# A hybrid attention and spectral kernel: the last stage placed inside the spectral stage, the rest loaded at once, columns loaded by GpSimd's queue, first matrices ahead of the token points

## The chip, the cores and the metric

The kernel runs on one core of one Trainium2 chip. The metric is the device time of one launch in microseconds (us). Each time is from one run; the median of three is compared. A profile is one execution recorded by the hardware profiler. Engines are named as the profile names them: PE is TensorE (PEld its weight loads), DVE is VectorE, ACT is ScalarE, POOL is GpSimd, SP is SyncE, which here only issues DMAs. ACT and POOL can issue DMAs as well.

## The reference

An image of 4 x 56 x 56 tokens with 128 channels passes a neighbourhood attention layer (group norm, 7 x 7 windows), a linear attention layer, and then a spectral layer, where the change lies. Cut to the spectral layer:

```python
t = t + attention(layer_norm(t))            # t: 4 x 3136 x 128
u = layer_norm(t)
for i, frac in enumerate((1, 2, 4, 8)):      # one of the four is selected by the weights
    ui = u[:, :T // frac]
    U_plus  = causal_fft_conv(phi, ui)       # 16 filters
    U_minus = sign * causal_fft_conv(phi, ui * sign)
    s_i = einsum('btkd,k,kde->bte', U_plus, sigma**0.25, M_phi_plus[i])
    s_i += einsum('btkd,k,kde->bte', U_minus, sigma**0.25, M_phi_minus[i])
    s_i += sum_j einsum('btd,de->bte', shift(ui, j), M_u[i, j])   # j = 0, 1, 2
out = t + sum_i weights[i] * pad(s_i)
```

All is float32.

## The kernel before

The program has three stages, one after the other: `layers` (both attention layers, the short shifts with M_u, and all preparation for the spectral layer), `spectral_layer`, and `onto_the_rest`. A second copy of all three stands in a branch that these inputs don't take.

`layers` leaves in HBM: `td`, the tokens with everything added but the spectral part (this is "the rest"); `xd`, the normalized tokens transformed along the image rows into 42 frequencies m1 (real and imaginary parts, and two shifts s); `vd`, the transformed filters; `wd`, the selected filter matrices (32 x 128 x 128). Its order is planned in Python by estimated costs and is then fixed on every engine.

`spectral_layer` goes over the 42 row frequencies, singly at both ends and in pairs between (`UNITS`). Four pieces of work make one frequency:

- Token points (L1490): `xm`, four loads from `xd` (L1478), is multiplied by the table `tok`. DVE, ACT and POOL copy the result into `us`, twelve planes (L1499 to L1503). Three `us` buffers are used in turn.
- Matrices (L1521): the 2 MB of `mats`, loaded once from `wd` by four DMAs on SP (L1433), times the filter points `v`, eight blocks t to a frequency. DVE and ACT copy them into `gt` (L1531).
- Products (L1541): `gt` times `us`, copied by ACT into `ys` (L1633). `ys` goes to `yd` in HBM and comes back regrouped as `yg` (L1554, L1560).
- Columns (L1569): `yg` times the table `back`, copied by ACT and DVE into `zs` (L182, L184), stored to `zd` in HBM by four DMAs on SP (L1584).

The function `step` writes the order on PE by hand: the matrices of the next unit are made between the products of the present one. For the very first unit there are no products: it makes the token points, and then all eight blocks of matrices. The results of the last frequency come after the last product.

The tables `v`, `tok` and `back` come in chunks of six frequencies on SP (L1463). SP works its list in order. A load into a buffer waits until the old content is used, and the DMAs of SP and ACT take eight semaphores in turn, so each also waits until the DMA that last had its semaphore has landed.

`onto_the_rest` transforms back along the rows. It opens its buffers when `spectral_layer` has closed its own. It clears `onto` and eight `z` buffers (four deep, two image halves q; L1687, L1697, DVE and POOL share the clearing), as the 84 rows that are loaded (partitions 0 to 83) are multiplied as 128. Then eleven steps of 1, 1, 2, 4, 4, 4, 4, 4, 2, 1, 1 image columns follow. In each, and for both halves:

- `tl`, the rest for these columns, is loaded from `td` by ACT (L1709), four buffers deep;
- `z` is loaded from `zd` by SP (L1711), 4 KB for each row and column;
- PE multiplies (L1719), four matmuls a column, each recorded twice;
- DVE masks and adds the result into `tl` (L1728), and ACT stores `tl` to the output (L1733).

In all, `z` is 19.3 MB, the rest 6.4 MB and the output 6.4 MB.

Of the kernel before, what the change touches and what calls it, by code (L numbers as in the profile page):

```python
# [57 lines left out]
NS, BR = 2, H // 2  # L58
N1, N2, NM = 42, W, W // 2
# [74 lines left out]
def hybrid_kernel(  # L134
# [39 lines left out]
    hmask = keep.tile([P, 1], F32, name="hmask")  # L174
# [1244 lines left out]
    def spectral_layer():  # L1419


        with ExitStack() as ph:
            tabs = ph.enter_context(tc.tile_pool(name="tabs", bufs=2))
            sp = ph.enter_context(tc.tile_pool(name="sp", bufs=2))
            sp1 = ph.enter_context(tc.tile_pool(name="sp1", bufs=1))
            ps_g = ph.enter_context(tc.tile_pool(name="ps_g", bufs=1, space=bass.MemoryType.PSUM))


# [1 line left out]
            mats = sp1.tile([P, NQE, GE // NQE, C], F32, name="mats")  # L1430
            by_group = wd.rearrange("k (t g i) d -> g k t (i d)", t=NQE, g=NG)
            for g in range(NG):
                nc.sync.dma_start(  # L1433
                    mats[32 * g : 32 * (g + 1)].rearrange("k t i d -> k t (i d)"), by_group[g]
                )

# [151 lines left out]
            def bank():  # L1588
                turn[0] = (turn[0] + 1) % 8
                return ps_g.tile([P, 512], F32, tag=f"g{turn[0]}", name="pg")  # L1590
# [19 lines left out]
            def step(s):  # L1610


                one = UNITS[s - 1] if s else []
                two = UNITS[s] if s < len(UNITS) else []
                turns = NM // 4
                free = MQ * len(one)

                order = list(range(free, NQE)) + list(range(free)) if two else []
                need = lambda t: -(-NMQ * (t + 1) // 4) if t < free else 0
                done = 0  # L1620

                def make():
                    if order and need(order[0]) <= done:
                        t = order.pop(0)
                        for n in range(len(two)):
                            matrices(s, t, n)

                def use(q, ns):

                    py = bank().rearrange("p (n c) -> p n c", c=C)  # L1630
                    for i, n in enumerate(ns):
                        product(py[:, i], s - 1, us_of(one[q]), q, n)
                    nc.scalar.copy(ys[:, ns[0] : ns[-1] + 1], py[:, : len(ns)])  # L1633

                if not one:
                    load_to(1)
                    points(0)
                    while order:
                        make()
                elif len(one) == 1 and two:  # L1640
                    ys = sp.tile([P, turns, C], F32, name="ys")
                    for n in range(turns):
                        make()
                        use(0, [n])
                        done += 1
                        if n == 3:
                            points(two[0])
                    ygs[one[0]] = regroup(one[0], ys)
                    make()
                    points(two[1])  # L1650
                else:
                    waiting = list(ygs)
                    for q in range(len(one)):
                        ys = sp.tile([P, turns, C], F32, name="ys")
                        for n in range(0, turns, 2):
                            last = n + 1 == turns
                            if last and q == 0 and two:
# [12 lines left out]
                assert not order  # L1670

            with tc.manual_schedule(engines={mybir.EngineType.PE}):
                for s in range(len(UNITS) + 1):
                    if s + 1 < len(UNITS):
                        tables_of(UNITS[s + 1][0])
                    step(s)
                for m1 in list(ygs):
                    results(m1)

    def onto_the_rest():  # L1680

        with ExitStack() as ph:
            fin = ph.enter_context(tc.tile_pool(name="fin", bufs=4, reuse_waits="tile"))
            ps_o = ph.enter_context(tc.tile_pool(name="ps_o", bufs=4, space=bass.MemoryType.PSUM))

            onto = fin.tile([P, NS, 64], F32, name="onto", bufs=1)
            nc.vector.memset(onto, 0.0)  # L1687
            nc.scalar.dma_start(
                onto[: 2 * N1, :, :H], table["onto"].rearrange("p (s h) -> p s h", s=NS)
            )  # L1690
            zs = [
                [fin.tile([P, 4, NS, B * C], F32, name=f"z{q}{i}", bufs=1) for q in range(2)]
                for i in range(4)
            ]
            for i in range(4):
                for q, e in enumerate((nc.vector, nc.gpsimd)):
                    e.memset(zs[i][q][64:], 0.0)  # L1697
            rows_in = td.rearrange("b (h w) c -> h b w c", w=W)
            rows_out = ot.rearrange("b (h w) c -> h b w c", w=W)

            steps = (1, 1, 2, 4, 4, 4, 4, 4, 2, 1, 1)
            assert sum(steps) == W // 2
            for n, wc in enumerate(steps):
                w0 = sum(steps[:n])
                tl = fin.tile([P, B, max(steps), C], F32, name="tl")
                zin = []
                for q in range(2):
                    ws = slice(q * BR + w0, q * BR + w0 + wc)
                    nc.scalar.dma_start(tl[64 * q : 64 * q + H, :, :wc], rows_in[:, :, ws])  # L1709
                    z = zs[n % 4][q]  # L1710
                    nc.sync.dma_start(  # L1711
                        z[: 2 * N1, :wc], zd[ws].rearrange("w p s b e -> p w s (b e)")
                    )
                    zin.append(z)
                for i in range(wc):
                    po = ps_o.tile([P, B, C], F32, name="po2")
                    for s in range(NS):
                        for q in range(2):
                            nc.tensor.matmul(  # L1719
                                po[64 * q : 64 * (q + 1)].rearrange("p b c -> p (b c)"),  # L1720
                                onto[:, s],
                                zin[q][:, i, s],
                                start=(s == 0),
                                stop=(s == NS - 1),
                            )
                    for q in range(2):
                        at = slice(64 * q, 64 * q + H)
                        nc.vector.scalar_tensor_tensor(  # L1728
                            tl[at, :, i], po[at], hmask[at], tl[at, :, i], ALU.mult, ALU.add
                        )  # L1730
                for q in range(2):
                    ws = slice(q * BR + w0, q * BR + w0 + wc)
                    nc.scalar.dma_start(rows_out[:, :, ws], tl[64 * q : 64 * q + H, :, :wc])  # L1733

    unfit = keep.tile([1, 1], mybir.dt.int32, name="unfit")
    layers(False, unfit)
    bad = nc.values_load(unfit)
    spectral_layer()
    onto_the_rest()
    with tc.If(bad > 0):  # L1740
        layers(True, None)
        spectral_layer()
        onto_the_rest()


# [52 lines left out]
```

## Time and profile before

| | us |
|---|---|
| median of 3 runs | 1634.19 (1628.76 to 1636.43) |
| the profiled execution | 1643.69 |
| its span, first to last instruction | 1641.8 |
| PE busy / DVE / ACT / POOL in it | 1436.1 / 1015.0 / 757.9 / 411.8 |
| spectral stage: first token load issued, last product starts | 757.53, 1486.23 |
| last columns (L1569) start | 1497.54 |
| first onto matmul (L1719), last one | 1518.25, 1635 |

The mean clock granted to PE is 0.939. Durations below are of the profiled execution, whose own time lies 9.5 us above the median of the runs. A line of a timeline has start, duration, engine, line, operation, and in brackets the idle time before it with what ended it. A line of the chain of waits has start, duration, and the instruction or wait that the chain passes through; "issue" is time for which the profile shows no cause. In the busy times by stage each engine has busy us and, in brackets, its number of instructions. "DMA share" is the mean busy share of 16 DMA engines; where packets overlap it can pass 1.

### The profile page before, as it was taken

What the parts mean: (1) busy time and instruction counts of PE and PEld (TensorE: products, weight loads), DVE (VectorE), ACT (ScalarE), POOL (GpSimd) and SP (SyncE); (2) the same over time, 40 slices, a digit from 0 to 9 for tenths busy, and PEclk for the clock granted to TensorE, in tenths of its full rate; (3) what the DMA queues carried; (4) which work ended last, traced back from release to release, by engine and by line L of the source; (5) the groups of instructions that cost most, each with busy time, mean ns of one, the idle gap of its engine ahead of it and who ended that gap; (6) DMA issues with size and microseconds to landing.
All of it is one profiled execution on the core that took longest, in us unless ns stands there. A gap on an engine that the chain in (4) does not pass through costs nothing.

```text
span 1641.8 us, 60848 instructions
## 1 busy us (share of the span) xinstructions
PE 1436.1 (87%) x26361; PEld 1115.2 (68%) x26361; DVE 1015.0 (62%) x2069; ACT 757.9 (46%) x1610; POOL 411.8 (25%) x813
## 2 busy tenths in 40 slices
PE   4887879889999999883999999999999999992566
PEld 3665658756876776562888888888888888880212
DVE  3775668777876777541766666666666666643324
ACT  2333445346635534342666655666566556640000
POOL 5135327433754464240010011001010101003000
PEclk9698999999999999996999999999999999995788
DMA  6455455744434244257144444444444454435997
GB/s 174 106 109 105 89 86 109 162 122 118 117 111 125 66 121 124 74 157 202 48 113 119 106 123 126 127 108 125 122 126 108 121 132 115 107 93 139 225 252 238
DMA packets 274388, 207.22 MB, mean 126 GB/s; under 512 B 104704, under 2 KB 241056, under 8 KB 274112
## 3 DMA queue, kind: packets, MB, share of 16 engines
q1 hardware_dynamic: 261154, 189.63, 45.1%
q10 hardware_dynamic: 12958, 13.61, 3.1%
q8 instruction: 209, 3.42, 0.9%
q14 instruction: 67, 0.55, 0.1%
HBM read 115.52 MB, written 87.64 MB: 124 GB/s over the span
## 4 chain that ended last, share of the span: by engine, by line
PE 66%; DMA 14%; POOL 7%; DVE 6%; SPq 4%; issue 2%; ACT 1%; POOLq 0%; DVEq 0%; ACTq 0%
PE pg L1521 18%; PE pg L1541 17%; PE pg L1490 5%; PE results L1185 4%; PE scores L1155 3%; PE pg L1569 3%; PE bk L828 3%; SPq L230 2%; DMA z<-zd 2%; DMA tl<-td 2%; DMA out_dram<-tl 2%; PE bk L887 2%; PE bk L733 2%; PE bk L703 2%; PE bk L501 2%
## 5 line engine op out<-in xcount | busy, mean ns | idle before, releaser
L1531 DVE COPY gt<-pg 128x448 f32<-128x448 f32 x672 | 372.9, 617 | 225.6 <-PE pg L1521 225.5
L1531 ACT COPY gt<-pg 128x448 f32<-128x448 f32 x672 | 313.6, 555 | 101.3 <-PE pg L1521 101.1
L1521 PE MATMUL pg<-v,mats 32*128 32x224 f32 (+1 forms) x5632 | 308.9, 356 | 0.0
L1541 PE MATMUL pg<-gt,us 128*32 128x128 f32 x9408 | 297.7, 277 | 1.3 <-DVE gt L1531 1.3
L1541 PEld LDWEIGHTS pg<-gt,us 128*32 128x32 f32 x9408 | 256.5, 138 | 51.8 <-DVE gt L1531 45.4
L1521 PEld LDWEIGHTS pg<-v,mats 32*128 32x128 f32 x5632 | 250.5, 187 | 30.0 <-issue 28.5
L1502 POOL COPY us<-us 128x448 f32<-128x448 f32 x42 | 23.5, 560 | 667.0 <-DVE us L1499 611.9
L1171 ACT ACTIVATE e<-scores 126x768 f32<-126x768 f32 (+1 forms) x140 | 107.6, 769 | 116.8 <-PE scores L1155 93.3
L1175 DVE TENSOR_TENSOR e<-e,relb 126x768 f32<-126x768 f32 (+1 forms) x140 | 138.1, 987 | 23.7 <-ACT e L1171 23.0
L1199 DVE RECIPROCAL recs<-results 128x96 f32<-128x96 f32 (+1 forms) x140 | 99.4, 710 | 55.1 <-PE results L1185 53.9
L1719 PE MATMUL po<-z,onto 128*64 128x512 f32 x224 | 76.6, 723 | 58.5 <-DMA z<-zd 57.4
L1155 PEld LDWEIGHTS scores<-qT,kp 32*126 32x126 f32 (+1 forms) x2240 | 75.3, 187 | 50.0 <-ACT e L1171 25.2
L1155 PE MATMUL scores<-qT,kp 32*126 32x96 f32 (+1 forms) x2240 | 98.2, 291 | 11.8 <-ACT e L1171 11.6
L1490 PE MATMUL pg<-tok,xm 56*128 56x56 f32 x1344 | 87.2, 278 | 24.3 <-DMA xm<-xd 24.3
L1633 ACT COPY ys<-pg 128x256 f32<-128x256 f32 (+1 forms) x171 | 58.6, 343 | 106.2 <-PE pg L1541 102.3
L1490 PEld LDWEIGHTS pg<-tok,xm 56*128 56x128 f32 x1344 | 81.5, 191 | 36.8 <-issue 25.4
L1719 PEld LDWEIGHTS po<-z,onto 128*64 128x64 f32 x224 | 25.3, 163 | 110.5 <-issue 75.9
L1499 DVE COPY us<-pg 128x448 f32<-128x448 f32 x84 | 48.5, 620 | 67.2 <-PE pg L1490 67.2
L1728 DVE SCALAR_TENSOR_TENSOR tl<-po,hmask,tl 56x512 f32<-56x512 f32 x56 | 42.0, 750 | 74.0 <-PE po L1719 73.3
L828 PE MATMUL bk<-mu,ut 128*112 128x128 f32 x672 | 82.3, 281 | 2.2 <-POOL ut L812 1.6
L1185 PE MATMUL results<-e,v_sb 126*32 126x96 f32 (+1 forms) x2240 | 76.1, 255 | 9.3 <-DVE aT L1200 9.3
L1214 POOL TENSOR_TENSOR total<-total,recs 128x448 f32<-128x448 f32 x28 | 31.7, 1134 | 206.4 <-DVE recs L1199 206.4
(176 smaller groups left out, 1969.1 us busy)
## 6 DMA issues: line engine op xcount, KB each, us to landing
xd<-xs SPq DMA_DIRECT2D x56, 336.0 KB
xm<-xd SPq DMA_DIRECT2D x168, 112.0 KB
yd<-ys SPq DMA_DIRECT2D x168, 112.0 KB
yg<-yd SPq DMA_DIRECT2D x168, 112.0 KB
zd<-zs SPq DMA_DIRECT2D x168, 112.0 KB
v_sb<-vpad SPq DMA_DIRECT2D x224, 63.0 KB
z<-zd SPq DMA_DIRECT2D x10, 1344.0 KB
acc<-in_x_dram SPq DMA_DIRECT2D x28, 224.0 KB
```

What stands on the lines that cost most here:

```text
L828: nc.tensor.matmul(pt[:CP, g * C : (g + 1) * C], ut[:, t0 : t0 + 2 * CP - 1 : 2], mu[:, i, :], start=(i == 0), stop=(i == NAR - 1),)
L1155: nc.tensor.matmul(sp[:, h, c * nq : (c + 1) * nq], keys_of(x0, y0 + c * KH, KH)[hs], qTs[b, ty][hs, QR * x0 : QR * x0 + nq], start=True, ...
L1171: nc.scalar.activation(e.rearrange("k (h q) -> k h q", h=NH), sp, AF.Exp)
L1175: nc.vector.tensor_tensor(e, e, relb[qc].rearrange("k h c q -> k (h c q)"), ALU.mult)
L1185: nc.tensor.matmul(po[hs, i, :nq], ones[:kn] if i else v_sb[:kn, c, hs], e[:, h, c], start=(c == 0), stop=(c == 1),)
L1199: nc.vector.reciprocal(rec, po[:, 1, :nq])
L1490: nc.tensor.matmul(pu[p][:, HALF * k : HALF * (k + 1)], xm[at, k % B, k // B, :], tok[at], start=True, stop=True,)
L1521: nc.tensor.matmul(pg[g][:, cols * i : cols * (i + 1)], mats[rows, t, ni * n + i, :], v[rows], start=True, stop=True,)
L1531: copy(rows_of(u + 1, t)[:, : MQ * nm, :, e0 : e0 + ni], pg[g][:, : cols * ni].rearrange("p (i q c) -> p q c i", i=ni, q=MQ * nm),)
L1541: nc.tensor.matmul(py[32 * j : 32 * (j + 1)], us.rearrange("p c k m -> p (c k) m")[:, NSB * FIRST[p, c] : NSB * (FIRST[p, c] + 4), 4 * n + j],
L1633: nc.scalar.copy(ys[:, ns[0] : ns[-1] + 1], py[:, : len(ns)])
L1719: nc.tensor.matmul(po[64 * q : 64 * (q + 1)].rearrange("p b c -> p (b c)"), onto[:, s], zin[q][:, i, s], start=(s == 0), stop=(s == NS - 1),)
```

## The change

The last stage moves into `spectral_layer`. The buffers `mats`, `gt` and `us` are in a pool of their own that is closed after the last `step`, and the buffers of the last stage are opened in its place, before the results of the last frequency. The rest is loaded whole, by fourteen DMAs on ACT with four columns each. Six `z` buffers (three deep) and `onto` are cleared by POOL over all 128 partitions, and filled in the middle, partitions 22 to 105. `z` is loaded by DMAs on POOL instead of SP. The matmuls use the spectral stage's PSUM banks. At the entry, `mats` is loaded by ACT instead of SP, and the first token points come after the first matrices. In the order of the changed program, ACT issues all fourteen loads of the rest after its last copy of a product and ahead of its copy for the last columns; POOL clears all buffers before it issues the first load of `z`.

```diff
-            sp1 = ph.enter_context(tc.tile_pool(name="sp1", bufs=1))
+            matrices_in = ph.enter_context(ExitStack())
+            sp1 = matrices_in.enter_context(tc.tile_pool(name="sp1", bufs=1))
...
-                nc.sync.dma_start(
+                nc.scalar.dma_start(
                     mats[32 * g : 32 * (g + 1)].rearrange("k t i d -> k t (i d)"), by_group[g]
                 )
...
                 if not one:
                     load_to(1)
-                    points(0)
                     while order:
                         make()
+                    points(0)
...
+            matrices_in.close()
+            fin = ph.enter_context(tc.tile_pool(name="fin", bufs=1, reuse_waits="tile"))
...
+            rest = fin.tile([P, B, BR, C], F32, name="rest")
+            half = [slice(64 * q, 64 * q + H) for q in range(2)]
+            for w0 in range(0, BR, 4):
+                for q in range(2):
+                    nc.scalar.dma_start(
+                        rest[half[q], :, w0 : w0 + 4], rows_in[:, :, q * BR + w0 : q * BR + w0 + 4]
+                    )
+            among = slice(P // 2 - N1, P // 2 + N1)
+            onto = fin.tile([P, NS, 64], F32, name="onto")
+            nc.gpsimd.memset(onto, 0.0)
+            nc.scalar.dma_start(
+                onto[among, :, :H], table["onto"].rearrange("p (s h) -> p s h", s=NS)
+            )
+            DEEP = 3
+            zin = [
+                [fin.tile([P, 4, NS, B * C], F32, name=f"z{q}{i}") for q in range(2)] for i in range(DEEP)
+            ]
+            for zs in zin:
+                for z in zs:
+                    nc.gpsimd.memset(z, 0.0)
+            with tc.manual_schedule(engines={mybir.EngineType.PE}):
                 for m1 in list(ygs):
                     results(m1)
...
-                tl = fin.tile([P, B, max(steps), C], F32, name="tl")
-                zin = []
                 for q in range(2):
-                    ws = slice(q * BR + w0, q * BR + w0 + wc)
-                    nc.scalar.dma_start(tl[64 * q : 64 * q + H, :, :wc], rows_in[:, :, ws])
-                    z = zs[n % 4][q]
-                    nc.sync.dma_start(
-                        z[: 2 * N1, :wc], zd[ws].rearrange("w p s b e -> p w s (b e)")
-                    )
-                    zin.append(z)
+                    nc.gpsimd.dma_start(
+                        zin[n % DEEP][q][among, :wc],
+                        zd[q * BR + w0 : q * BR + w0 + wc].rearrange("w p s b e -> p w s (b e)"),
+                    )
                 for i in range(wc):
-                    po = ps_o.tile([P, B, C], F32, name="po2")
+                    po = bank()
...
-                            tl[at, :, i], po[at], hmask[at], tl[at, :, i], ALU.mult, ALU.add
+                            rest[half[q], :, w0 + i],
+                            po[half[q]].rearrange("p (b c) -> p b c", b=B),
+                            hmask[half[q]],
+                            rest[half[q], :, w0 + i],
+                            ALU.mult,
+                            ALU.add,
```

More of the change, by code (lines that the diff above doesn't have):

```diff
@@ L1676, in spectral_layer @@
                     step(s)
+            matrices_in.close()
+            fin = ph.enter_context(tc.tile_pool(name="fin", bufs=1, reuse_waits="tile"))
+            rows_in = td.rearrange("b (h w) c -> h b w c", w=W)
+            rows_out = ot.rearrange("b (h w) c -> h b w c", w=W)
+            rest = fin.tile([P, B, BR, C], F32, name="rest")
[5 more added lines that the diff above has]
+                    )
@@ L1677, in spectral_layer @@
+            with tc.manual_schedule(engines={mybir.EngineType.PE}):
                 for m1 in list(ygs):
                     results(m1)
[L1680 to L1689, printed above, removed]
-            )
[L1691 to L1699, printed above, removed]
@@ L1701, in onto_the_rest @@
             steps = (1, 1, 2, 4, 4, 4, 4, 4, 2, 1, 1)
-            assert sum(steps) == W // 2
+            assert sum(steps) == BR
             for n, wc in enumerate(steps):
                 w0 = sum(steps[:n])
-                tl = fin.tile([P, B, max(steps), C], F32, name="tl")
-                zin = []
                 for q in range(2):
-                    ws = slice(q * BR + w0, q * BR + w0 + wc)
-                    nc.scalar.dma_start(tl[64 * q : 64 * q + H, :, :wc], rows_in[:, :, ws])
-                    z = zs[n % 4][q]
-                    nc.sync.dma_start(
-                        z[: 2 * N1, :wc], zd[ws].rearrange("w p s b e -> p w s (b e)")
+                    nc.gpsimd.dma_start(
+                        zin[n % DEEP][q][among, :wc],
+                        zd[q * BR + w0 : q * BR + w0 + wc].rearrange("w p s b e -> p w s (b e)"),
@@ L1719, in onto_the_rest @@
                             nc.tensor.matmul(
-                                po[64 * q : 64 * (q + 1)].rearrange("p b c -> p (b c)"),
+                                po[64 * q : 64 * (q + 1)],
                                 onto[:, s],
-                                zin[q][:, i, s],
+                                zin[n % DEEP][q][:, i, s],
                                 start=(s == 0),
@@ L1726, in onto_the_rest @@
                     for q in range(2):
-                        at = slice(64 * q, 64 * q + H)
                         nc.vector.scalar_tensor_tensor(
-                            tl[at, :, i], po[at], hmask[at], tl[at, :, i], ALU.mult, ALU.add
+                            rest[half[q], :, w0 + i],
[4 more added lines that the diff above has]
+                            ALU.add,
                         )
                 for q in range(2):
-                    ws = slice(q * BR + w0, q * BR + w0 + wc)
-                    nc.scalar.dma_start(rows_out[:, :, ws], tl[64 * q : 64 * q + H, :, :wc])
+                    nc.scalar.dma_start(
+                        rows_out[:, :, q * BR + w0 : q * BR + w0 + wc], rest[half[q], :, w0 : w0 + wc]
+                    )
     unfit = keep.tile([1, 1], mybir.dt.int32, name="unfit")
@@ L1738, in hybrid_kernel @@
     spectral_layer()
-    onto_the_rest()
     with tc.If(bad > 0):
@@ L1742, in hybrid_kernel @@
         spectral_layer()
-        onto_the_rest()
 def kernel(**inputs):
```

## The prediction

> **What bounds the kernel now.** I read the page's slices and chain first, then the chain of waits in two windows, then busy times by stage. In the long middle the tensor engine is full; I left it, since no edit enters it. Two places are not: the entry to the spectral stage, and all that follows its last product.
>
> The chain of waits, in order of time, at the entry (start us, us, what):
>
> ```profile
> 753.78 11.37 DMA mats<-wd
> 765.15 0.02 issue
> 765.17 4.77 DMA xm<-xd
> 769.94 0.14 issue
> 770.07 3.63 PE pg L1490 x30
> 773.70 6.59 PE pg L1521 x132
> ```
>
> The matrices land at 765.15. Then a token load has to land, then the token points are made, and only at 773.7 does the first matrix product start.
>
> The chain at the end:
>
> ```profile
> 1497.54 3.10 PE pg L1569 x8
> ...
> 1504.27 3.52 POOL z L1697
> ...
> 1508.20 9.80 DMA z<-zd
> ...
> 1596.22 22.36 DMA tl<-td
> ```
>
> The last columns come at 1497.5, buffers are cleared until 1507.8, and from there DMAs carry the chain. Busy time by stage shows what they do (stretch, us, engines, TensorE clock, DMA share, GB/s):
>
> ```profile
> 1484.00:1502.00 18.00, 7.22 (x48) 2.30 (x46) 1.52 (x3) 1.44 (x3) 1.18 (x1) 0.50 0.31 78
> 1502.00:1508.00 6.00, 0.00 (x0) 0.00 (x0) 3.47 (x1) 0.00 (x0) 6.00 (x3) 0.50 0.60 163
> 1540.00:1560.00 20.00, 11.91 (x40) 4.75 (x40) 6.00 (x8) 0.00 (x0) 0.00 (x0) 0.83 0.93 236
> 1580.00:1600.00 20.00, 12.13 (x35) 3.70 (x36) 6.00 (x8) 0.00 (x0) 0.00 (x0) 0.87 0.91 255
> ```
>
> From 1508 on the DMAs run at a share above 0.9 while TensorE is busy 60%: the last stage is bound by bytes. From 1484 to 1502 they stand at 0.31. The same stage in forty slices, from 1500 to 1642:
>
> ```profile
> GB/s 66 207 184 170 251 251 211 192 211 226 224 227 228 175 247 308 228 203 191 250 277 299 297 286 300 285 185 198 288 291 298 233 199 162 317 263 158 290 306 49
> ...
> q1 hardware_dynamic: 5292, 19.73, 51.4%
> q10 hardware_dynamic: 10654, 12.89, 33.0%
> ```
>
> The rate swings between about 290 and 160 to 200. SP's queue (q1) moves 19.73 MB in 5292 packets (3.7 KB each: z), ACT's (q10) 12.89 MB in 10654 (1.2 KB: tl and out). I take z at 295 GB/s and the rest at 195: 19.3/0.295 + 12.85/0.195 = 65 + 66 = 131 us, from 1508 to 1639. The span ends at 1641.8, so these two rates explain the stage, with no idle time inside it to win. Who SP waits for in that window says the same from the other side:
>
> ```profile
> SPq L1711 <- DMA tl<-td: 44.4, 5, 17.7
> SPq L1711 <- DMA out_dram<-tl: 36.6, 6, 10.5
> ```
>
> A load of z has nothing to do with tl. The DMAs of SP and ACT share eight semaphores in turn, so each waits until the one that had its semaphore before has landed. This matters below.
>
> [...] SP was held 81 us by other DMAs and the rate stayed at its level. So GpSimd's queue is no gain in bandwidth. [...]
>
> **The change, part by part** (on the profiled execution: span 1641.8 us, own time 1643.69).
>
> 1. Matrices loaded by ACT. The four loads still wait until the last xd<-xs has landed (751.7), as their buffer lies on xs. SP's v, tok and back no longer queue behind them, and start earlier. But by the order of semaphores mats 3 waits for back, and mats 4 for the fourth xm, which stands behind an xm that waits for mats 1. Estimate: mats 1 lands at 756, that xm at 760, mats 4 is issued at 760.5 and needs 0.52 MB at 0.21 plus 2 us: 765. By bytes: 2.1 MB + 0.9 MB of xm + some 0.4 MB of tables at 0.21 from 751.8 is 768. I take 766, bounds 762 and 771 (before: 765.15). Behind the waiting loads on ACT stand its first copies of gt, which need the matrices anyway: free.
>
> 2. First matrices ahead of points(0). Before: from 773.63 to 786.74 TensorE does nine blocks of matrices, bound by the copies (16 on DVE in 8.73 us), then the first product. After: the same 13.1 us start at 766; between them come the points, 2.0 us at full clock as in L1490 later (32 in 1.93), and the product waits for the copies of us: DVE 1.16, then three POOL copies of 0.56, about 2.5 us, of which the ninth block hides 1.7. So 766 + 13.1 + 2.0 + 0.8 = 781.9 against 786.74: 4.8 us gained, bounds 0 and 9. The next token load, on SP behind the points, is needed 25 us later: free.
>
> 3. rest loaded at once. It lies where mats and gt lay, so ACT issues it when the last product is done, 1488.6: 14 loads, 6.42 MB, all in runs of 2 KB, where tl had 512 B and 1 KB in its small steps; 6.42/0.20 = 32 us. Beside it run the last columns: yd, yg and zd, DMA time 0.31 x 18 = 5.6 us, which were free before. They are late now. One yd waits for rest 1; each hop of 2 to 2.6 us (1478.09 and 1480.61 in the chain) about doubles: +6, so the last columns come at 1503. ACT's last copy of zs stands behind all 14 issues, but these end when yg has landed and rest 7 is in, some 1506. The real wait is on SP: the four last zd stores use the semaphores of rest 8 to 11, and so wait for eleven of fourteen loads: 1488.6 + 2 + 11 x 2.3 + 4 = 1520. They land by 1523, so z starts at 1523.5, where it was 1507.8. The remaining 1.4 MB of rest fill the gap, until 1527.
>
> 4. Clears: seven on POOL, six of 3.5 us, from 1488.3 to 1510. Hidden under the loads of rest, which last until 1520; without that cover they would cost the 2 us by which they pass 1507.8. ACT waits only for the first, small one.
>
> 5. z by GpSimd's queue, three buffers deep. The price of issue is unknown. Below nothing: z is no longer held by the shared semaphores, up to 5 us of smoother mixing. Above: 22 issues. [...] I take 1. Nothing but later z loads stands behind a waiting one on POOL. Depth: a step of four columns is 2.75/0.295 + 0.92/0.195 = 14 us of DMA, TensorE needs 10 to 12 for it (12.26 and 10.13 in the trace), so the load three steps on is issued about as the next one lands, with another still queued: no hole.
>
> Sum at the end: DMA work from 1488.6 is 32 + 5.6 + 65 + 33 = 136 us, plus 1 for GpSimd and 2.8 for the tail (1639 to 1641.8): 1628. Gain 14 us, bounds 4 (rest and columns in each other's way for 10 us more) and 22. With part 2: 19 us; I round to 18 of 1641.8. The median shown is 9.5 below the profiled time; from it, 1634 - 18 = 1616.
>
> **Rivals.** (a) Slower: the issue of z on GpSimd becomes the bound. Place: POOL after 1523.5, 4704 rows of 4 KB in 22 loads, one queue in order. It decides from about 98/4704 = 21 ns per row, 7 us for a load of 336 rows. At 30 ns it is 141 us: the end comes 43 us later than at the bound, 1616 + 43 = 1659. For: no row of the profile prices it. [...] (b) The columns lose what rest gains: the DMAs are full either way, zd is held to 1535 and TensorE, z and out start with nothing left to overlap; gain at the end 2, at the entry 4: 1628. For: the semaphore chain of part 3. Against: rest fills the wait. (c) The entry gives nothing, as mats 4 lands at 771: 1620. (d) Freed of the shared semaphores the mix runs at 280 GB/s instead of 255: 25.7 MB save 9 us: 1607.
>
> **Numbers.** Forecast with (c): 0.53; (d) 0.08; (b) 0.20; (a) 0.19. About 0.5% (8 us) is what this kernel's measurement tells from no change. Faster takes the forecast, (c) and (d): 0.61; same, (b): 0.20; slower, (a): 0.19. Range 1600 to 1654: below it half of (d), above it half of (a). The likeliest case's own range is 1606 to 1626.
>
> **What would show it** (by the line numbers of before). L1490 after the first L1521; first L1521 at 762 to 771; first L1541 near 782. rest from 1484 on at a share above 0.8; zd stores near 1513 to 1520; first onto matmul near 1528 instead of 1518; then z and out at 255 GB/s without holes. Wrong if POOL's DMA issues stand back to back while the DMA share falls, if the first z lands after 1540, or if mats lands after 775.

## The result and the profile after

| | before | after |
|---|---|---|
| median of 20 runs each, same chip | 1635.92 (1628.76 to 1642.99) | 1632.6 (1625.1 to 1639.55) |
| after / before, 95% interval | | 0.9975 (0.9959 to 0.999) |
| profiled execution, span | 1641.8 | 1627.0 |
| last `xd<-xs` landed | 751.72 | 741.56 |
| from there to the first product | 35.0 | 36.7 |
| first product to the end of the last | 701.4 | 701.0 |
| end of the last product to the end | 153.6 | 147.8 |

The forecast was 1616, a gain of 18 us; the medians show 3.3. The spans differ by 14.8 us, but 10.2 of that lies ahead of the changed code: the last `xd<-xs` landed anywhere from 735.9 to 751.7 us in the profiles of this study. So I read only stages that are counted from that landing. In this pair of profiles they lose 1.7 us at the entry and gain 5.8 at the end: 4.1 us, in line with the medians.

The chain of waits of the changed kernel at the entry (start us, us, what):

```profile
737.14 4.42 DMA xd<-xs
...
741.66 8.16 DMA mats<-wd
...
750.18 6.01 DMA xm<-xd
756.19 0.02 issue
756.21 6.18 DMA mats<-wd
762.39 0.04 issue
762.44 6.74 PE pg L1523 x101
...
778.29 1.04 PE pg L1543 x32
```

The fourth matrices load is issued at 756.2, 14.6 us after the landing, because a token load and before it the first matrices load had to land. The matrices are complete 20.8 us after the landing (13.4 before). From there to the first product (L1543) are 15.8 us (21.6 before, from 765.15 to 786.74): the new order does save its time, and the late matrices take it back.

The same view at the end:

```profile
1480.23 7.01 DMA zd<-zs
...
1487.25 7.47 DMA yd<-ys
...
1495.99 8.22 DMA yg<-yd
...
1504.66 13.19 DMA onto<-onto
1517.85 0.34 issue
1518.19 0.82 POOL z L1716
...
1573.11 30.65 DMA z<-zd
1603.76 0.04 issue
1603.80 16.32 PE pg L1724 x56
```

The hops over `yd` and `yg`, 2 to 2.6 us before, take 7.5 and 8.2 beside the loads of the rest. POOL waits until 1518.2, 38.9 us after the last product. The chain names the load of `onto` as what let it go, and that is not so. POOL's semaphore waits at this line (count, then shortest, median and longest in ns, first and last start):

```profile
L1716 POOLq EVENT_SEMAPHORE  x20: 17/17/37820, 1479.6 to 1606.1; - x20
```

The longest is the first, from 1479.6 to 1517.4. The trace has the last store of `zd`, issued at 1511.3, landing at 1517.35, and `onto` only at 1517.85, when POOL had done its semaphore waits. So z waited for the stores of the last columns.

The last large load of z takes 30.7 us; when it lands, TensorE still has seven columns to do (56 recorded matmuls) and needs 16.3 us for them.

Busy time by stage (stretch, us, then PE, PEld, DVE, ACT and POOL busy with their counts, TensorE clock, DMA share, GB/s):

```profile
1481.00:1490.00 9.00, 0.00 (x0) 0.00 (x0) 0.00 (x0) 0.00 (x0) 9.00 (x4) 0.57 0.94 262
1500.00:1510.00 10.00, 3.48 (x8) 0.60 (x8) 0.69 (x1) 0.58 (x1) 0.32 (x1) 0.50 0.93 213
1510.00:1518.00 8.00, 0.00 (x0) 0.00 (x0) 0.00 (x0) 0.00 (x0) 0.00 (x0) 0.50 0.74 199
1518.00:1598.00 80.00, 56.87 (x166) 18.24 (x167) 29.90 (x40) 0.00 (x0) 13.29 (x20) 0.90 1.01 250
1598.00:1627.00 29.00, 17.56 (x59) 5.75 (x57) 12.10 (x17) 0.00 (x0) 1.03 (x2) 0.80 0.71 202
```

The DMAs are busy at once (0.94 where it was 0.31). But then z and the output move at only 250 GB/s, with the DMAs full at 1.01, and in the last 29 us the share drops to 0.71. The queues from 1500 to the end (packets, MB, share of 16 engines' time in the window) and who SP waited for from 1478 to 1530:

```profile
q0 software_dynamic: 5728, 19.27, 62.5%
q10 hardware_dynamic: 6913, 9.32, 26.6%
q1 hardware_dynamic: 403, 0.80, 2.1%
```

```profile
SPq L1586 <- DVE zs L184: 16.3, 2, 10.8
SPq L1562 <- DMA yd<-ys: 7.1, 3, 5.0
...
SPq L1586 <- DMA rest<-td: 1.6, 1, 1.6
```

z now comes through GpSimd's queue, q0. The stores of `zd` (L1586) wait for the columns, and hardly (1.6 us) for the semaphores of the rest.

### The profile page after: what moved, and what is told of

The parts are those of the page before. It is cut to its first block, busy times and chain, and to the rows that moved or that the text cites. A ratio compares the mean times of both kernels' runs of the same rounds, so it can differ in the third digit from the quotient of the medians.

```text
span 1627.0 us, 60816 instructions
## 1 busy us (share of the span) xinstructions
PE 1437.5 (88%) x26361; PEld 1117.7 (69%) x26361; DVE 1002.5 (62%) x2064; ACT 757.6 (47%) x1610; POOL 431.6 (27%) x838
## 4 chain that ended last, share of the span: by engine, by line
PE 66%; DMA 13%; DVE 7%; POOL 6%; issue 4%; SPq 3%; ACT 1%; ACTq 0%; DVEq 0%; POOLq 0%
PE pg L1523 18%; PE pg L1543 17%; PE pg L1492 5%; PE results L1185 4%; PE scores L1155 3%; PE bk L828 3%; DMA z<-zd 3%; PE pg L1571 3%; SPq L230 3%; PE bk L887 2%; PE bk L501 2%; DVE e L1175 2%; PE bk L733 2%; POOL hna L547 1%; PE bk L703 1%
## 5 line engine op out<-in xcount | busy, mean ns | idle before, releaser
L1523 PE MATMUL pg<-v,mats 32*128 32x224 f32 (+1 forms) x5632 | 312.3, 357 | 25.6 <-DMA mats<-wd 25.5
L1543 PE MATMUL pg<-gt,us 128*32 128x128 f32 x9408 | 297.4, 277 | 1.3 <-DVE gt L1533 1.3
L1543 PEld LDWEIGHTS pg<-gt,us 128*32 128x32 f32 x9408 | 256.4, 138 | 51.9 <-DVE gt L1533 45.7
L1724 PE MATMUL pg<-z,onto 128*64 128x512 f32 x224 | 74.4, 667 | 39.4 <-DMA z<-zd 39.4
L1732 DVE SCALAR_TENSOR_TENSOR rest<-pg,hmask,rest 56x512 f32<-56x512 f32 x56 | 42.0, 750 | 72.5 <-PE pg L1724 71.9
L1724 PEld LDWEIGHTS pg<-z,onto 128*64 128x64 f32 x224 | 24.0, 148 | 90.6 <-issue 67.2
L828 PEld LDWEIGHTS bk<-mu,ut 128*112 128x112 f32 x672 | 80.0, 191 | 4.0 <-POOL ut L812 1.9
## 6 DMA issues: line engine op xcount, KB each, us to landing
z<-zd POOLq DMA_DIRECT2D x10, 1344.0 KB, 28.1
```

Of the source, the lines that this page charges most:

```text
L828: nc.tensor.matmul(pt[:CP, g * C : (g + 1) * C], ut[:, t0 : t0 + 2 * CP - 1 : 2], mu[:, i, :], start=(i == 0), stop=(i == NAR - 1),)
L1523: nc.tensor.matmul(pg[g][:, cols * i : cols * (i + 1)], mats[rows, t, ni * n + i, :], v[rows], start=True, stop=True,)
L1543: nc.tensor.matmul(py[32 * j : 32 * (j + 1)], us.rearrange("p c k m -> p (c k) m")[:, NSB * FIRST[p, c] : NSB * (FIRST[p, c] + 4), 4 * n + j],
L1724: nc.tensor.matmul(po[64 * q : 64 * (q + 1)], onto[:, s], zin[n % DEEP][q][:, i, s], start=(s == 0), stop=(s == NS - 1),)
```

## Experiments

Two suspects came from these lines: ACT's queue for the matrices, and GpSimd's queue for z. All ratios below are to the kernel before, on the same chip, with 95% intervals. "Entry" is from the last landing of `xd<-xs` to the first product, "last stage" from the end of the last product to the end, both of the profiled execution.

| run | matrices by | points | z by | ratio | entry | last stage |
|---|---|---|---|---|---|---|
| before | SP | first | SP | 1 | 35.0 | 153.6 |
| changed | ACT | after | POOL | 0.9975 (0.9959 to 0.999) | 36.7 | 147.8 |
| changed, again (e12) | ACT | after | POOL | 0.9966 (0.995 to 0.9983) | 35.4 | 147.4 |
| e1_mats_sp | SP | after | POOL | 0.9934 (0.9906 to 0.9962) | 30.6 | 147.8 |
| e2_end_only | SP | first | POOL | 0.9942 (0.9922 to 0.9961) | 36.0 | 147.9 |
| e3_rest_after | ACT | after | POOL | 0.9976 (0.9958 to 0.9993) | 37.2 | 150.2 |
| e4_z_sp | ACT | after | SP | 0.9897 (0.986 to 0.9935) | 33.7 | 138.4 |
| e5_before_z_pool | SP | first | POOL | 1.0101 (1.0066 to 1.0136) | 34.5 | 174.2 |
| e6_both_sp | SP | after | SP | 0.9861 (0.9824 to 0.9898) | 30.4 | 139.4 |
| e7_z_half | ACT | after | both | 0.9951 (0.9936 to 0.9966) | 37.6 | 149.0 |
| e8_mats_pool | POOL | after | POOL | 0.9943 (0.9922 to 0.9963) | 33.6 | 148.2 |
| e9_twos | ACT | after | POOL | 0.991 (0.9877 to 0.9943) | 34.0 | 140.3 |
| e10_rest_late | SP | after | SP | 0.9903 (0.9864 to 0.9941) | 29.2 | 146.8 |
| e11_points_first | SP | first | SP | 0.9926 (0.9902 to 0.995) | 35.3 | 138.6 |
| e13_sp_twos | SP | after | SP | 0.9865 (0.9832 to 0.9899) | 28.8 | 133.5 |
| e14_short_tail | ACT | after | POOL | 0.9923 (0.9897 to 0.995) | 36.5 | 142.1 |
| e15_twos_three | ACT | after | POOL | 0.9925 (0.99 to 0.9951) | 35.4 | 140.2 |

The stages come from one profile each. How far one can be trusted is seen where the same part was profiled again: the last stage of the changed kernel is 147.4 to 148.2 us in the five runs that leave it alone, the entry with ACT's matrices 33.7 to 37.6 in eight. The gain that the two stages add up to and the one of the ratio lie up to 6 us apart (e7), mostly within 4.

### The entry: who loads the matrices, and the order of the points

```diff
-                nc.scalar.dma_start(
+                nc.sync.dma_start(
                     mats[32 * g : 32 * (g + 1)].rearrange("k t i d -> k t (i d)"), by_group[g]
                 )
```

> The changed kernel with the four matrices loads back on SP's queue; the order of points and matrices stays as changed. Theory A (ACT's loads lose time to the shared DMA semaphores: mats waits for a token load which itself waits for mats): the last matrices land 13 to 14 us after the last xd<-xs instead of 20.8, the first product starts 29 to 30 us after it instead of 36.7, and the kernel is 7 us faster than the changed one, about 1625 where before is 1635 (0.994 of before). Theory B (the loads land late because of the bytes that stand beside them, whoever issues them): mats again near 20 us, time as the changed kernel, 0.9975 of before.

Measured: 0.9934, entry 30.6 us. Theory A's size, on the profile and in the times. The chain of waits of this run:

```profile
739.91 4.02 DMA xd<-xs
...
746.00 0.61 SPq L1435
...
746.65 11.72 DMA v<-vd
...
758.52 6.96 PE pg L1523 x122
...
774.59 1.04 PE pg L1543 x32
```

SP issues all four within 2.7 us of the landing; they and the tables that follow are there at 758.4, 14.5 us after it, instead of 20.8.

The second run also puts the points back to the front:

```diff
+                    points(0)
                     while order:
                         make()
-                    points(0)
```

> Both entry edits undone (matrices on SP, token points ahead of them), so only the last stage is changed. Theory A: entry as before, first product 35 us after the last xd<-xs; the last stage, from the last product to the end, takes about 148 us instead of 153.6, so the kernel is 6 us faster than before (0.9965), 1 to 2 us faster than the changed one. If the last stage brought the 14 us of the prediction and the entry lost 10, it would be 0.991.

Measured: entry 36.0 and last stage 147.9, as Theory A has them; the ratio, 0.9942, is 0.2% better than it said, and its interval holds 0.996 but not 0.9965. The stage sums put this run level with the changed one. What the medians add to that I can't explain; nothing below rests on it.

Were ACT's matrices late by the shared semaphores, or by the traffic beside them? GpSimd's queue, whose 22 DMAs in the trace of the changed kernel carry semaphores of their own (111 to 118, where the 1466 of SP and ACT carry 100 to 107), was to tell:

```diff
-                nc.scalar.dma_start(
+                nc.gpsimd.dma_start(
                     mats[32 * g : 32 * (g + 1)].rearrange("k t i d -> k t (i d)"), by_group[g]
                 )
```

> The changed kernel with the matrices loaded by GpSimd's queue, whose DMAs have semaphores of their own. Theory A (on ACT mats was late because of the semaphores shared with SP's token loads): the last matrices land 14 to 16 us after the last xd<-xs as on SP, first product 30 to 32 us after it, 5 to 7 us faster than the changed kernel. Theory B (it is late because the token loads and tables, no longer queued behind it, take DMA time beside it): mats near 18 to 21 us as on ACT, no gain.

Measured: in between. All four are issued by 744.9; the chain says

```profile
744.91 15.26 DMA mats<-wd
```

so they are complete at 760.2, about 18 us after the last landing (the first token load, which waits for it, is issued at 742.2). With ACT the last matrices landed 18.5 to 21.8 us after that landing in eight profiles, on SP 13.0 to 14.1 in the four whose chain of waits has them; in the other four with SP, matrices and tables were there after 13.6 to 14.6. So this one run lies just below ACT's range and 4 us above SP's, though all four loads were issued within 3 us of the landing: most of the delay remains without the chain of semaphores, beside token loads and tables. That is Theory B's landing; that the chain costs anything besides is not shown, as 0.4 us below the range is no more than scatter. And as GpSimd's queue itself proved slower for z (below), the share of the traffic may be smaller than these 4 us.

The same edit of the points' order alone, in the kernel with both queues on SP:

> The kernel with matrices and z on SP, with the token points again ahead of the first matrices (that edit alone undone). Theory A: the first product comes 35 to 36 us after the last xd<-xs instead of 30.4, 4.5 to 5.5 us slower, 0.989 to 0.990 of before. Theory B (the order of points gives nothing): same as with it, 0.986.

Measured: entry 35.3 instead of 30.4, the 4.9 us of Theory A. The ratio, 0.9926 instead of 0.9861, moved by some 10 us, more than the stage, and 0.990 lies just outside its interval; with few runs of either I go by the stage. Taken over all profiles: 29.8 us with SP and points after (four runs, 28.8 to 30.6), 35.2 with SP and points first (four, 34.5 to 36.0), 35.8 with ACT and points after (eight, 33.7 to 37.6). The order is worth 5.4 us, and ACT's queue costs 6.0.

### The last stage: which queue loads z

```diff
-                    nc.gpsimd.dma_start(
+                    nc.sync.dma_start(
                         zin[n % DEEP][q][among, :wc],
```

> The changed kernel with z loaded by SP's queue instead of GpSimd's. Theory A (the stage is bound by bytes, the issuing engine does not matter): within 3 us of the changed kernel. Theory B (on SP the z loads share their semaphores with the out stores and wait for them): 4 to 10 us slower, with SP waiting for out<-rest. Theory C (GpSimd's own path writes its rows slowly): 4 us or more faster.

Measured: 0.9897, last stage 138.4 us: Theory C, and more than I thought. SP does wait for other DMAs' semaphores (28.1 us for `out_dram<-rest`), and is still the better queue. First the 80 us from the start of z in this run, by stage, with the rest of it; then the queues of these 80 us, here and in the changed kernel:

```profile
1521.00:1601.00 80.00, 59.95 (x177) 18.99 (x178) 30.11 (x41) 0.00 (x0) 0.00 (x0) 0.90 0.89 273
1601.00:1622.00 21.00, 12.08 (x48) 4.11 (x46) 11.89 (x16) 0.00 (x0) 0.00 (x0) 0.91 0.58 189
```

```profile
q1 hardware_dynamic: 4595, 17.82, 74.6%
```

```profile
q0 software_dynamic: 4818, 16.37, 85.5%
```

273 GB/s at a share of 0.89, against 250 at 1.01. Each MB of z takes 0.746 x 16 x 80 / 17.82 = 53.6 us of DMA-engine time on SP's queue and 66.9 on GpSimd's. Packets overlap (a share of 1.01 is above 1), so part of that is time beside others: the output on ACT's queue, which no edit touched, went from 46.3 to 53.6 us for each MB in the same windows (3.98 MB at a share of 14.4%, 3.56 MB at 14.9%). The GB/s are the firmer number. GpSimd's has more small packets too: z in pieces of 4096 bytes would be 3997 packets for 16.37 MB, and there are 821 more; on SP's queue 244 more than 4351.

The opposite edit in the kernel before, at its L1711:

```diff
-                    nc.sync.dma_start(
+                    nc.gpsimd.dma_start(
                         z[: 2 * N1, :wc], zd[ws].rearrange("w p s b e -> p w s (b e)")
```

> The kernel before with one edit: its z loads are issued by GpSimd instead of SP (four buffers deep, all else as before). Theory A (z on GpSimd's queue costs DMA time: 66 us of DMA-engine time per MB in the changed kernel's last stage against 53 on SP's queue with the same loads): 7 to 11 us slower than before, 1.004 to 1.007, and more packets than bytes/4096 on the software queue. Theory B (the 9 us lie in the changed kernel's depth of three, or in rest, not in the queue): same as before within 3 us, or faster, since SP was held by tl and out.

Measured: 1.0101, 16.5 us slower, with nothing else of the change, and more than the 7 to 11 us expected. The busy time of the first 80 us of z, before and in this run:

```profile
1508.00:1588.00 80.00, 40.73 (x116) 14.28 (x118) 29.91 (x29) 0.00 (x0) 6.68 (x2) 0.73 0.92 238
```

```profile
1507.00:1587.00 80.00, 48.37 (x128) 14.79 (x128) 24.48 (x27) 0.00 (x0) 13.06 (x20) 0.86 1.03 216
```

Again 9% fewer bytes at a higher share. Four buffers deep, a load of 1344 KB took 58.1 us to land (median of the four recorded from 1520 on). But this run's time is not the rate alone. From its chain of waits, and from the waits of 1500 to 1655:

```profile
1537.17 35.75 DMA out_dram<-tl
DVE tl L1728 <- DMA tl<-td: 45.9, 6, 17.3
```

z is no longer held by the DMAs of the output and of `tl` (81.0 us of SP's waits before, nothing in POOL's waits of this run), and these two now come late: the longest store of the chain takes 35.8 us (18.1 before), the loads of `tl` wait for the stores, and DVE waits 45.9 us for `tl`, of which there is nothing before. How the 16.5 us divide was not measured.

Half of z on either queue:

```diff
-                    nc.gpsimd.dma_start(
+                    (nc.sync, nc.gpsimd)[q].dma_start(
                         zin[n % DEEP][q][among, :wc],
```

> The changed kernel with the z loads of the first half (q = 0) on SP and those of the second half on GpSimd. Theory A (cost by the byte on GpSimd's queue): half of the 9 us comes back, last stage 142 to 145 us, 4 to 5 us faster than the changed kernel, 0.993 to 0.995. Theory B (what counts is that GpSimd, not held by the other DMAs' semaphores, has three steps of loads under way at once, so that each lands late): with half of them let loose it stays nearer to 147 or falls all the way to 139, and the software queue's time per MB differs from the changed kernel's.

Inconclusive. The times (0.9951) agree with half of the 9 us, the profile (149.0) does not: an output store took 46.1 us to land, and in the chain of waits the next load of SP's half was issued only behind it, at 1589.3. A MB took 67.7 us of DMA time on q0 and 62.2 on q1 in the same 80 us.

### Rate or size: what of the 9 us is the queue

Smaller loads, on GpSimd's queue as changed:

```diff
-            DEEP = 3
+            DEEP = 6
-                [fin.tile([P, 4, NS, B * C], F32, name=f"z{q}{i}") for q in range(2)] for i in range(DEEP)
+                [fin.tile([P, 2, NS, B * C], F32, name=f"z{q}{i}") for q in range(2)] for i in range(DEEP)
-            steps = (1, 1, 2, 4, 4, 4, 4, 4, 2, 1, 1)
+            steps = (1, 1, 2, 2, 2, 2, 2, 2, 2, 2, 2, 2, 2, 2, 1, 1)
```

> The changed kernel with its steps of four columns cut to steps of two and z in six pairs of buffers of two columns, in the same memory; z stays on GpSimd's queue (32 loads instead of 22). Theory A (GpSimd's queue costs by the byte): last stage as in the changed kernel within 3 us, 0.996 to 1.000 of before. Theory B (loads of 1.3 MB, three steps at once, land so late that TensorE is left with 16 us of work at the end): the tail shortens, last stage 139 to 143 us, 0.990 to 0.994.

Measured: 0.991, last stage 140.3: Theory B. The rate over the first 80 us stays at 254 GB/s:

```profile
1519.00:1599.00 80.00, 57.75 (x180) 17.32 (x180) 31.10 (x42) 0.00 (x0) 20.75 (x32) 0.95 1.00 254
```

The end changes, since after the last wait for z TensorE has 7.1 us of matmuls left instead of 16.3. With loads of four columns SP's queue has a short end too: 1.9 us in e4, 2.4 in e6. So the queue's rate was not all of its 9 us. Three runs were to separate the two. The first has this edit together with the two one-line edits that put the matrices and z on SP:

> The kernel with matrices and z on SP, with steps of two columns and six pairs of buffers as in e9_twos. Theory 1 (GpSimd's queue moves fewer bytes in the same time): over the first 80 us of z 270 GB/s or more against 254 in e9_twos, last stage 133 to 137 us against 140.3; 0.981 to 0.985 of before. Theory 2 (size and number of loads alone): the last stage as in e9_twos, 139 to 141 us, the rate too; 0.985 to 0.988.

Measured: last stage 133.5 us, and 301 GB/s over the first 80 us:

```profile
1513.00:1593.00 80.00, 64.79 (x216) 20.49 (x216) 40.42 (x54) 0.00 (x0) 0.00 (x0) 0.96 0.88 301
```

With the size held at two columns, the queue is worth 6.8 us (140.3 to 133.5): Theory 1 for the stage. At the 295 and 195 GB/s of the prediction, the 18.61 MB of z and 5.44 MB of output in these 80 us would take 91. The ratio, 0.9865, stayed above the 0.981 to 0.985 expected; 0.985 is within its interval.

The second changes one line of the changed kernel:

```diff
-            steps = (1, 1, 2, 4, 4, 4, 4, 4, 2, 1, 1)
+            steps = (1, 1, 2, 4, 4, 4, 4, 2, 2, 2, 1, 1)
```

> The changed kernel with only its last step of four columns cut in two (24 loads of z instead of 22), z on GpSimd's queue. Theory 2 (the last large load leaves TensorE 16 us of work after the last wait for z): after that wait 8 to 11 us of matmuls, last stage 142 to 144 us instead of 147.5; 0.993 to 0.995 of before. Theory 1: as the changed kernel, 147 us, 0.9966 to 0.998.

Measured: last stage 142.1, 0.9923: Theory 2, with less left at the end than the 8 to 11 us it said. The end of its chain of waits:

```profile
1604.53 8.92 DMA z<-zd
1613.45 0.04 issue
1613.49 1.95 PE pg L1724 x6
```

One load cut in two, and 2 us of matmuls are left after the last wait instead of 16.

And the third is e9_twos with

```diff
-            DEEP = 6
+            DEEP = 3
```

> e9_twos with three pairs of buffers instead of six: z on GpSimd's queue in steps of two, at most 4 MB under way. If the lower rate comes from the amount under way, the first 80 us of z go at 270 GB/s; if from the queue, at 250 to 255 or less, since TensorE's waits for z then leave holes. Last stage 140 to 146 us, 0.991 to 0.996.

Measured: 140.2 us, 0.9925, and 263 GB/s:

```profile
1522.00:1602.00 80.00, 60.69 (x182) 18.84 (x184) 31.71 (x43) 0.00 (x0) 19.80 (x30) 0.87 1.01 263
```

Half of the amount under way moves the rate by 9 GB/s, hardly more than the scatter of this rate (246 to 257 in six runs on GpSimd's queue with four columns in all loads, or all but the last); the queue moves it by 18 to 47 (216 against 238 in the kernel before, 250 against 268 to 280 in the changed one, 254 against 301 in steps of two). So both readings hold: GpSimd's queue moves fewer bytes in the same time, and large loads that land together leave TensorE the last word. From the changed kernel's 147.8, SP's queue alone gives 9.0 us, steps of two alone 7.5, both together 14.3: they overlap, as SP's queue shortens the end as well.

### The rest: is its early load worth anything

```diff
-            for w0 in range(0, BR, 4):
-                for q in range(2):
-                    nc.scalar.dma_start(
-                        rest[half[q], :, w0 : w0 + 4], rows_in[:, :, q * BR + w0 : q * BR + w0 + 4]
...
                 for m1 in list(ygs):
                     results(m1)
+            for w0 in range(0, BR, 4):
+                for q in range(2):
+                    nc.scalar.dma_start(
+                        rest[half[q], :, w0 : w0 + 4], rows_in[:, :, q * BR + w0 : q * BR + w0 + 4]
```

> The changed kernel with the 14 rest loads issued after the last columns' copy instead of at the last product. Theory A (the early load fills DMA time that was idle, but puts the yd and yg hops off by 11 us): the last columns come 9 to 10 us after the last product instead of 23.5, z starts near 21 us after it (end of the clears) instead of 39, and rest then takes its 28 us beside z; from the last product to the end 150 to 154 us instead of 147.7, so 2 to 6 us slower than the changed kernel. Theory B (what rest gains the columns lose): same end within 2 us.

This did not ask the question: in the order that came out on ACT, seven of the fourteen loads still went ahead of the columns. Times as changed (0.9976), last stage 2.4 us longer. The next run has the order on ACT written out too, in the kernel with both queues on SP:

```diff
-            with tc.manual_schedule(engines={mybir.EngineType.PE}):
+            with tc.manual_schedule(engines={mybir.EngineType.PE, mybir.EngineType.Activation}):
                 for m1 in list(ygs):
                     results(m1)
+                for w0 in range(0, BR, 4):
...
```

> The kernel with matrices and z on SP (0.986 of before), with the rest loads held until after the copy of the last columns, ACT's order written out. Theory A (the early load of rest is the gain of the last stage, as it fills 30 us in which the DMAs were at a third): z starts 21 to 23 us after the last product instead of 37.6, but all of rest then stands beside z, and the last stage takes 149 to 153 us instead of 139.4: 0.992 to 0.995 of before. Theory B (rest's early load only puts off the columns; the gain over the kernel before lies in longer packets and earlier clears): 138 to 142 us, 0.985 to 0.988.

Measured: last stage 146.8 instead of 139.4, 0.9903 instead of 0.9861. z is issued at 1491.9, 23.1 us after the last product instead of 37.6, and still the end comes 7.4 us later. Theory A in direction; its size was a little high.

### Both queues on SP, and the changed kernel again

The first of these has the one-line edits of e1_mats_sp and e4_z_sp together, the second no edit.

> The changed kernel with both the matrices and z on SP's queue: the order of points, the early rest and the clears stay. Theory A (the two changes of queue are what cost the expected gain, and they add): first product 30 us after the last xd<-xs, last stage 138 to 139 us from the last product, 0.985 to 0.987 of before, about 1614. Theory B (they do not add, a bound common to both stands behind): 0.989 or more.

Measured: 0.9861, entry 30.4, last stage 139.4, median 1612.71 us beside 1638.4 before. The two edits add. In the stages the kernel beats either alone; in the times its interval and that of e4 overlap. In steps of two (e13) the last stage is 5.9 us shorter still, but the times, 0.9865, are level.

> The changed kernel once more, unaltered, beside the others on one chip, as their common measure: 0.996 to 0.999 of before if its first measurement holds; if 0.994, the runs with one edit (0.9934 to 0.9951) lie nearer to it than their difference from 0.9975 says.

Measured: 0.9966. Both measurements put the changed kernel 3 to 5 us below the one before.

## Why the prediction was wrong

The sum was 4.8 us at the entry and 14 at the end. Two of its terms were mis-sized: the landing of ACT's matrices, by 6 us, and the price of GpSimd's queue for z, by 9. Of the others, the new order of the points and the clears held; the term of the early rest came out right because two of its errors cancel, which is luck.

1. Matrices by ACT, "I take 766, bounds 762 and 771", that is 14.3 us after the last landing (upper bound 19.3): wrong in size. They were complete 20.8 us after it, beyond the bound, and 18.5 to 21.8 over eight profiles, two of them within it. The chain I named is there link by link: first matrices load, token load, fourth matrices load. But the links took 8.2, 6.0 and 6.2 us where I put 4 to 5 each: I priced each as if alone, while matrices, eight token loads and tables ran beside each other. Cost: 6.0 us over the profiles, more than the whole gain of the entry. This is rival (c)'s place, with an even later landing.
2. First matrices ahead of the points, 4.8 us: right, 5.4 over the profiles.
3. The rest loaded at once: the gain is there, the way to it was told wrongly. z did wait for the last `zd` stores, but these were held by the columns, not by the semaphores of the rest (1.6 us): I gave the hops over `yd` and `yg` 6 us more in all, and they took 11. The last store then took 6 us to land where I put 3. z started 38.9 us after the last product instead of 34.9. Against that the loads beside the columns moved at 226 GB/s from 1481 to 1510 (6.6 MB in 29 us) where I put 200, and z and the output moved at 268 to 280 GB/s on SP's queue, where my sum implies 262 (25.7 MB in 98 us). On SP the last stage is 138.4 to 139.4 us in three runs; the prediction's end, 1628, less 1488.6, where it has the last product end (the trace has 1488.2), is 139.4. That match is the luck of the later start against the higher rate.
4. Clears: right; POOL clears until 1500.3 and then waits for the columns.
5. z by GpSimd's queue, "I take 1": this is the term that failed most, by 9.0 us (147.8 on GpSimd's queue over five runs, 138.8 on SP's over three). I priced its issue, and its issue is cheap: 22 instructions of 0.5 to 0.8 us, never in the way, so rival (a)'s mechanism, POOL as the bound, did not occur. The 1 us was my estimate; no trace stood behind it. What it costs is rate, which I set equal on all queues: 273 against 250 GB/s over 80 us are 1.84 MB, by my estimate 6.7 us at the higher rate, and with two-column loads the queue measured 6.8. The remainder of the 9.0 I put to the longer end. The equal rate was my assumption: that SP was held 81 us and the rate stayed at its level says nothing of how many bytes another queue moves, and the trace of before has no DMA from GpSimd. "Depth ... no hole" was wrong for the tail: 16.3 us of matmuls after the last large load had landed. And that the stage had no idle time to win was fitted, not shown: the two rates were chosen to give its length, and e13 beat them.

Rival (b), 1628, came closest in time, but by luck: its mechanism, that the columns lose what the rest gains, is not what happened, as the early rest is worth 7.4 us of the last stage. Rival (d)'s smoother mix came true with the opposite queue. For the move of z to partitions 22 to 105 I put 0, an estimate: no run tried it alone. Why GpSimd's queue moves fewer bytes stays open: the extra small packets are shown, that they are the cause is not. Taking z to another queue also takes it out of the shared semaphores, which changes what stands beside it; halving the amount under way (e15) speaks against that as the whole cause, but no run separates the two.

## What to carry to other kernels

Here, with the DMAs as the bound, the queue of a transfer had a rate of its own (250 against 273 GB/s) besides the price of its instructions (0.5 to 0.8 us each on GpSimd's): measure the GB/s of the same stage with the transfer on either queue, and busy share x 16 x window / MB beside it, before moving it for good. The size of the last loads set what compute remained after them (16.3 us of matmuls, 2.0 with the last step of four cut in two); cut the last step first (here 5.7 us). And when loads move to a queue that shares semaphores with another, follow the chain of "waits for the one before last" with durations taken under the traffic that the move itself lets loose.

## What was not expected of the hardware

- z by GpSimd's queue: 66.9 us of DMA-engine time per MB against 53.6 on SP's queue (1 MB here 10^6 bytes), with 821 packets beyond 4096-byte pieces in 16.37 MB against 244 in 17.82. In the kernel before it was 216 against 238 GB/s; the 16.5 us that it lost there come in part from output stores and loads of `tl` that landed late beside z, up to 35.8 us after their issue.
- A summed DMA share above 0.9 does not mean equal throughput: 1.01 carried 250 GB/s and 0.89 carried 273.
- Two-column loads of z on SP's queue moved at 301 GB/s, with four-column loads at 268 to 280.
- The hops to `yd` and back as `yg`, four DMAs of 112 KB each way, grew from 2.1 and 2.6 us to 7.5 and 8.2 beside 14 loads of 448 KB.
